# A four-layer attention stack on one core: the order of 2673 tasks from a written list instead of from a ranked greedy planner

## The chip, the cores and the metric

One core of a Trainium2 chip runs the whole program. The metric is the device time of one execution in microseconds (us). Engines are named as in the profile: PE is the matrix engine (PEld its weight loads), DVE the vector engine, ACT the scalar engine with its function tables, POOL the GpSimd engine, SP the engine that issues most transfers.

## The reference, cut to what matters

Four attention layers follow one another on a batch of 4 sequences of 256 rows by 256 columns, float32; the context `ctx` is a second input of the same size.

```python
# layer 0, twice: heads of 128, 16 heads, one learned extra key and value
h = layer_norm(x); q, k, v = h @ wq + bq, ctx @ wk + bk, ctx @ wv + bv      # 256 x 2048 each
x = x + softmax(q k^T / sqrt(128)) v @ wo + bo
x = x + gelu(layer_norm(x) @ w_fc1 + b_fc1) @ w_fc2 + b_fc2                 # 256 -> 1024 -> 256
# layer 1: 16 heads of 16 over ctx, then an MLP with tanh-gelu
# layer 2: the latents are x, keys and values from ctx and x (512 keys), 16 heads of 16, a mask, rms norm, MLP
# layer 3: 32 query heads of 8 over 8 key heads, a mask, projection, layer norm -> out
```

The four sequences (batches b = 0 to 3) depend on one another nowhere; within a batch everything is a chain.

## The kernel before, in words

The kernel is written as a list of tasks. `Task` (line 174) is one short stretch of PE work (or none), followed by its `posts`: pieces of work on DVE, ACT, POOL or SP that read what PE left in PSUM, each with an estimated duration. A task names what it comes `after`, and the buffers that it `takes` from and `gives` back to rings (`Ring`, line 144). The ring `PS` (line 198) holds the eight PSUM banks, shown in the profile as `ps_pj`, `ps_s`, `ps_et` and `ps_o`, two of each. There are 2673 tasks, 1547 of them with PE work.

PE work has three shapes. "full" uses the whole array. "rows" (queries against keys with heads of 16 or 8) uses 32 rows of the array for each matmul, and a task fills two of the four row strips; two such tasks with different strips can be issued as a pair, interleaved, so that four matmuls run side by side. "cols" (weights times values of those heads) uses 32 columns each, four at a time.

Stages, in the names of the code:

- Stage 0, layer 0. `norm` (line 246: statistics on DVE, a power on POOL as `root`, `apply` on DVE), `transposed`, then for four groups of four heads: `seven` (line 1090, the projections, each 2x2 block product done with seven products instead of eight, in four PE tasks `first` to `fourth`, with sums of operands made ahead on POOL: `sums`, `value_sums`, `wo_sums`), `scores` with a maximum on DVE and an exponential on ACT, `quotients` (line 1468: one reciprocal and four scalings of the tile `E` on DVE), `turns` (transposes of `E` with a copy by ACT to `eT`), `weighted` (to `cT`), `tile_sums` (line 1532: four additions on `cT` and `sc`, on DVE or POOL) and `products` (line 1547, the output projection: the first task `t1` needs no `tile_sums`, the second, `t2`, does), each added to the tile `X` by DVE.
- Stages 1, 3 and 5: the MLPs. `up` needs a GELU table in ACT, everything else of ACT the EXP table.
- Stages 2, 4: layers 1 and 2 (`unit16`, line 670): `maxima` (rows, with a DVE maximum into the tile `shift`), `turns`, `weights` (rows, with exponentials on ACT), `weighted` (cols), `ending`.
- Stage 6: layer 3 (`unit8`, line 579): `scores` (rows, with a DVE operation that adds the mask and takes the maximum), `exps` on ACT, `turns` with a copy by ACT or DVE, `weighted`, `ending`, projection, and `closing` (line 923: statistics, root, two DVE operations, the output transfer).

`plan` (line 1728) walks through the tasks once in Python, before the program is built, with one clock for each engine. At each step it looks at all tasks whose predecessors are done and whose buffers are free, ranks them by the longest remaining chain less handicaps by batch and by kind (`HANDICAPS`, line 1852) and takes the best of those that would start soonest. It pairs two "rows" tasks where it can. For a post that may go to either of two engines it takes the one that would end first. The steps are then emitted in that order (line 1892), and `Pinned` (line 126) keeps every engine's instructions in the order of emission: nothing is reordered later. On the chip each engine works through its own list in order, and waits only for data and for buffers. Since all instructions pass through `Pinned`, they all carry line 134 in the profile; tiles tell them apart.

The lines that keep DVE and POOL apart in the plan: a post marked `near` that lands on DVE is made longer by the time for which POOL is busy.

Of the kernel before, what the change touches and what calls it, by code (L numbers as in the profile page):

```python
# [51 lines left out]
def kernel(ctx: ExitStack, tc: tile.TileContext, a: dict, out: bass.AP):  # L52
# [193 lines left out]
    def norm(b, after, src, eps, mean, st, take=()):  # L246
# [39 lines left out]
        t = Task(b, None, 0, None, [t], posts=[Post(("POOL",), 300, root)], lag=0.1)  # L286
# [77 lines left out]
    def attention(L, b, after, hTs, dst, dst_after, weights_at, before):  # L364
# [214 lines left out]
        def unit8(t, q):  # L579
            u = {}  # L580
            S_tasks, V_tasks = [], []
            for j in range(4):
# [5 lines left out]
                for pair in range(2):  # L588
# [12 lines left out]
                    def least(e, i, v=v):  # L601
# [10 lines left out]
                        b, "rows", 0.87, scores, [grab], takes=takes, pair=pair,  # L612
# [6 lines left out]
                    for i in range(2):  # L619
# [5 lines left out]
                        def turns(i=i, v=v):  # L625
                            for kc in range(2):
# [10 lines left out]
                                b, "full", 0.49, turns, [tx], takes=[(PS, v, ("t", i))],  # L637
# [32 lines left out]
        def unit16(t, q):  # L670
# [3 lines left out]
            for g in range(2):  # L674
                Ms = []
                grab = Task(b, None, 0, None, ready[t], takes=[(SHIFTS[g], q["shift"], g)])
                for q0 in range(0, 2, per):
                    for pair in range(2):
# [13 lines left out]
                        def most(e, i, g=g, q0=q0, pair=pair, v=v):  # L692
# [8 lines left out]
                                b, "rows", 0.87, maxima, [grab], pair=pair,  # L701
# [24 lines left out]
            for kc in range(NCK):  # L726
# [5 lines left out]
                for pair in range(2):  # L732
# [13 lines left out]
                    def exps(e, i, kc=kc, pair=pair, v=v):  # L746
# [7 lines left out]
                            b, "rows", 0.87, weights, [grab], pair=pair, takes=[(PS, v, 0), (PS, v, 1)],  # L754
# [168 lines left out]
    def closing(b, after):  # L923

        for i in range(2):
# [20 lines left out]
            t = Task(b, None, 0, None, [t], posts=[Post(("POOL",), 300, root)], lag=0.1)  # L946
# [143 lines left out]
    def seven(b, after, A, sum_, block, T, to, bias, row=None):  # L1090
# [62 lines left out]
        def last(gives):  # L1153
# [18 lines left out]
        t2 = Task(b, "full", 0.86, second, [t1], takes=[(UU, u, 1), (HALFWAY, u, "in")], posts=saved(1, 0, 1, 0))  # L1172
        t3 = Task(
            b, "full", 1.73, third, [t2], takes=[(PS, v, 2), (UU, u, 2)],
# [3 lines left out]
            b, "full", 1.73, fourth, [t3], gives=[(HALFWAY, u, "in")],  # L1178
# [47 lines left out]
    for li in range(2):  # L1226
# [35 lines left out]
        for hg in range(NG):  # L1262
# [54 lines left out]
            for bp in range(2):  # L1317
# [112 lines left out]
                for bb in range(2):  # L1430
# [46 lines left out]
                    for h in range(HG):  # L1477
# [3 lines left out]
                        def turns(h=h, v=v, E=E):  # L1481
# [8 lines left out]
                            b, "full", 0.44, turns, tN, takes=[(PS, v, "pt"), (ET, y, "eT")],  # L1490
# [41 lines left out]
                    def tile_sums(e, c=c, sc=sc):  # L1532
# [11 lines left out]
                        posts=[Post(("DVE", "POOL"), {"DVE": 1400, "POOL": 3100}, tile_sums, near=True)],  # L1544
# [15 lines left out]
                    def add(i, j, at_, b=b, v=v, gives=()):  # L1560
                        def run(e):
                            to = Xb(b)[:, i, j * P : (j + 1) * P]
                            ve.tensor_tensor(to, v["pt"][2][:, at_ * P : (at_ + 1) * P], to, ALU.add)

                        return Post(("DVE",), 215, run, gives=gives)

                    t1 = Task(
                        b, "full", 0.88, products((0, (0, 0), (0, 0), True), (1, (0, 1), (1, 0), False)),
                        tC + [t_w["wo"], t_plus[b]], takes=[(PS, v, "pt")], posts=[add(0, 0, 0), add(0, 0, 1)],
                    )  # L1570
                    t2 = Task(b, "full", 0.44, products((0, 0, 0, False)), [t1, t_sc, t_tw], posts=[add(1, 0, 0)])

                    t3 = Task(
                        b, "full", 0.88, products((0, (1, 0), (0, 1), False), (2, 1, 1, False)), [t2],
# [3 lines left out]
                        b, "full", 0.88, products((0, 2, (1, 1), False), (2, (1, 1), 2, False)), [t3],  # L1578
# [136 lines left out]
    for t in reversed(tasks):  # L1715
        t.level = t.us + sum(p.us for p in t.posts) + t.lag + 0.25
        t.level += max((n.level for n in t.then + t.hinted), default=0.0)
    TURN = {"full": 0.1, "rows": 0.2, "cols": 0.14}
    LATE, TABLE, HELD = 0.2, 1.3, 1.0
    TAIL = {"DVE": 0.085, "ACT": 0.12, "POOL": 0.1, "SP": 0.0}  # L1720
    rings = {r for t in tasks for r, _, _ in t.takes} | {r for t in tasks for r, _, _ in t.gives}
    needs = {}
    for t in tasks:
        needs[t] = {}
        for r, _, _ in t.takes:
            needs[t][r] = needs[t].get(r, 0) + 1

    def plan(handicap):

# [4 lines left out]
        table, shape, held = EXP, None, False  # L1734
# [3 lines left out]
        by_batch, by_kind, (near, slack, solo, wide) = handicap  # L1738
        rank = {t: t.level - by_batch[t.stage][t.b] - by_kind.get((t.stage, t.kind), 0) for t in tasks}
        order = {t: i for i, t in enumerate(tasks)}  # L1740
        count = {t: len(t.after) + len(t.behind) for t in tasks}
        open_ = [t for t in tasks if not count[t]]
        ready = {t: 0.0 for t in open_}

        def earliest(t):

            if held and any(p.table not in (None, table) for p in t.posts):
                return None
            when = ready[t]
            for r, n in needs[t].items():  # L1750
                w = r.when(n)
                if w is None:
                    return None
                when = max(when, w)
            return when

        def do(group, start):
            nonlocal table, shape, held
            taken = []
            for t in group:  # L1760
                for r, h, k in t.takes:
                    h[k] = r.take()
                    taken.append((r, h, k, h[k][1]))
            end = start
            if group[0].shape:
                end = start + max(t.us for t in group)
                clock["PE"], shape = end, group[0].shape
                end += LATE
# [5 lines left out]
            for t, p in queue:  # L1774
                def ends(e):
                    more = TABLE if e == "ACT" and p.table not in (None, table) else 0.0
                    begin = max(clock[e], end)
                    if p.near and e == "DVE":
                        more += HELD * min(max(clock["POOL"] - begin, 0.0), p.ns[e])
                    return begin + more + p.ns[e] * wide  # L1780
# [11 lines left out]
            for t in group:  # L1792
                t.done += t.lag
                for r, h, k in t.gives:
# [3 lines left out]
                held = held if t.holds is None else t.holds  # L1798
                open_.remove(t)
                for n in t.then:  # L1800
                    count[n] -= 1
                    if not count[n]:
                        open_.append(n)
                        ready[n] = max([d.done + near for d in n.after], default=0.0)
            steps.append((group, taken, behind))

        def wait(t, w):
            switch = any(p.table not in (None, table) for p in t.posts)
            return max(w - clock["PE"], 0.0) + (TABLE / 2 if switch else 0.0)

        while open_:
            found = [(t, earliest(t)) for t in open_]
            found = [(t, w) for t, w in found if w is not None]
            if not found:
                return None
            best, products = None, []
            for t, w in found:
                if not t.shape:
                    continue
                turn = TURN[t.shape] if t.shape != shape else 0.0  # L1820
                idle = wait(t, w) + turn
                if t.shape != "rows":
                    products.append((idle, max(w, clock["PE"]) + turn, [t]))
                    continue
                for o, v in found:
                    if o.shape != "rows" or o.pair == t.pair or o.pair < t.pair:
                        continue
                    both = [w, v]
                    for r, n in needs[t].items():
                        both.append(r.when(n + needs[o].get(r, 0)))  # L1830
                    if None in both:
                        continue
                    both = max(both)
                    products.append((max(wait(t, both), wait(o, both)) + turn, max(both, clock["PE"]) + turn, [t, o]))
                products.append((idle + solo, max(w, clock["PE"]) + turn, [t]))
            if products:
                least = min(p[0] for p in products) + slack
                best = max((p for p in products if p[0] <= least), key=lambda p: (max(rank[t] for t in p[2]), -p[0]))
            others = [
                (max(w, clock["PE"], *(clock[p.engines[0]] for p in t.posts if p.engines[0] in ("POOL", "SP"))), -rank[t], order[t], t, w)  # L1840
                for t, w in found if not t.shape
            ]
            if others and (best is None or min(others)[0] <= best[1]):
                _, _, _, t, w = min(others)
                do([t], w)
            else:
                do(best[2], best[1])
# [4 lines left out]
    HANDICAPS = (  # L1852
        [
            [527, 717, 992, -701],
            [-9576, 3530, 999, -8122],
            [355, 669, -1239, 5671],
            [542, 1381, -2079, 2561],
            [-979, -2578, -4331, 417],
            [-1355, 7177, 208, -5575],
            [-677, -12218, 4083, 3351],  # L1860
        ],
        {
            (0, "columns.run"): -45, (0, "columns.scaled"): -58, (0, "context_sums.run"): -13,
            (0, "differences.run"): 122, (0, "exp"): 23, (0, "fetch.run"): -18, (0, "learned"): -54,
            (0, "norm.apply"): 29, (0, "norm.root"): 408, (0, "norm.stats"): 49, (0, "plus_row_to.run"): 12,
            (0, "products.run"): 9, (0, "quotients"): 13, (0, "rest_of.<lambda>"): -54, (0, "rows_of.<lambda>"): 65,
            (0, "run"): 3, (0, "scores"): 124, (0, "seven.first"): -1, (0, "seven.fourth"): 416,
            (0, "seven.second"): 124, (0, "seven.third"): 11, (0, "sums.run"): 2572, (0, "tile_sums"): 12,
            (0, "transposed.run"): -596, (0, "turns"): -615, (0, "value_sums.run"): 74, (0, "weighted"): 1704,
# [92 lines left out]
```

## Time and profile before

| | |
|---|---|
| median of 3 runs | 1338.98 us (1338.95 to 1340.37) |
| the profiled execution's own time | 1339.38 us |
| its span, first to last instruction | 1337.6 us |
| outside the span | 1.8 us |
| PE busy | 1300.0 us, 97% of the span |
| DVE busy | 873.2 us, 65% |
| ACT busy | 706.4 us, 53% |
| POOL busy | 266.0 us, 20% |
| granted PE clock | 0.999 |
| moved from and to HBM | 38.08 MB, mean 28 GB/s |

The profiled execution is 0.4 us above the median. The ends of matmuls are modelled and overlap the next ones, so that PE shows as busy in part of the time in which it is held up; the starts of matmuls tell more. A float32 matmul has two records in the trace, a transpose one, so 5143 instructions give 8907 records. The records of each engine stand in the order of the list, so every one of them can be put to its task.

### The profile page before, as it was taken

Reading aid. Unit: us, or ns where it says so; the run is one execution under the profiler, and the core shown is the slowest. Engines: PE = TensorE matmul, PEld = TensorE weight load, DVE = VectorE, ACT = ScalarE, POOL = GpSimd, SP = SyncE. Lnnn points to the kernel's source line nnn. Section 1 sums busy time; section 2 is a strip of 40 time slices with the busy share of each in tenths; the row PEclk is TensorE's granted clock in tenths of the full one; section 3 lists DMA queues with packets and bytes.
Section 4 is the critical chain, followed back from the end, with each engine's and each line's share of the span. In section 5 each row is a group of like instructions: output and inputs, shape, how many; then the busy total and the mean of one; then the engine's idle time right before and its main releaser. Section 6 shows DMA issues by size and latency. Waiting matters only on the chain.

```text
span 1337.6 us, 23607 instructions
## 1 busy us (share of the span) xinstructions
PE 1300.0 (97%) x8907; PEld 1038.3 (78%) x8907; DVE 873.2 (65%) x2431; ACT 706.4 (53%) x1689; POOL 266.0 (20%) x447
## 2 busy tenths in 40 slices
PE   8899999999999999999999999999999999999997
PEld 4788888888978888888898876658666667576764
DVE  6867757776687667676672577571772376556786
ACT  3554544544444535455363145545435687668986
POOL 8500304003241040120114341101220110020000
PEclk9999999999999999999999999999999999999999
DMA  7110200102001011010014110000000000000000
GB/s 235 33 32 1 79 1 17 64 1 79 1 16 64 1 35 46 1 48 1 11 59 142 39 49 5 1 1 5 5 5 1 1 1 1 17 1 9 2 9 17
DMA packets 25633, 38.08 MB, mean 28 GB/s; under 512 B 2244, under 2 KB 16086, under 8 KB 25392
## 3 DMA queue, kind: packets, MB, share of 16 engines
q1 hardware_dynamic: 24640, 35.56, 8.3%
q0 software_dynamic: 608, 0.76, 0.5%
q8 instruction: 70, 1.15, 0.4%
q14 instruction: 43, 0.35, 0.1%
q10 hardware_dynamic: 272, 0.26, 0.1%
HBM read 35.52 MB, written 1.05 MB: 27 GB/s over the span
## 4 chain that ended last, share of the span: by engine, by line
PE 86%; DVE 9%; ACT 3%; issue 1%; DMA 1%; SPq 0%; POOL 0%; DVEq 0%; ACTq 0%
PE ps_pj L134 22%; PE ps_et L134 22%; PE ps_s L134 21%; PE ps_o L134 21%; DVE E L134 1%; DVE eq L134 1%; ACT eq L134 1%; DMA bvl<-in_cols_dram 1%; DVE sc L134 1%; DVE qk L134 1%; ACT qk L134 1%; DVE X L134 1%; DVE shift L134 1%; DVE u L134 0%; ACT e L134 0%
## 5 line engine op out<-in xcount | busy, mean ns | idle before, releaser
L134 ACT ACTIVATE eq<-eq,nm 128x256 f32<-128x256 f32 x256 | 106.2, 505 | 0.0
L134 DVE TENSOR_SCALAR E<-E,rinv 128x257 f32<-128x257 f32 x256 | 96.6, 440 | 2.2
L134 PE MATMUL ps_s<-qk 32*128 32x256 f32 (+1 forms) x282 | 81.6, 474 | 1.0 <-ACT qk L134 0.6
L134 PE MATMUL ps_o<-qk 32*128 32x256 f32 (+1 forms) x270 | 76.5, 456 | 0.4 <-ACT qk L134 0.4
L134 POOL TENSOR_TENSOR X<-X,rowbc 128x256 f32<-128x256 f32 x56 | 41.3, 757 | 157.2 <-PE ps_et L134 69.6
L134 PE MATMUL ps_et<-qk 32*128 32x256 f32 (+1 forms) x258 | 70.8, 449 | 0.0
L134 PE MATMUL ps_pj<-qk 32*128 32x256 f32 (+1 forms) x214 | 63.0, 460 | 0.0
L134 POOL TENSOR_SCALAR mv<-mv 128x2 f32<-128x2 f32 (+1 forms) x32 | 7.5, 235 | 238.8 <-DVE mv L134 238.3
L134 DVE TENSOR_REDUCE shift<-ps_s 128x1 f32<-128x512 f32 (+1 forms) x62 | 41.8, 684 | 11.7 <-PE ps_s L134 5.0
L134 PE MATMUL ps_o<-eq,qk 32*128 32x256 f32 x216 | 47.3, 401 | 0.8 <-ACT e L134 0.8
L134 PE MATMUL ps_pj<-eq,qk 32*128 32x256 f32 x196 | 47.9, 401 | 0.0
L134 PE MATMUL ps_et<-eq,qk 32*128 32x256 f32 x204 | 47.0, 401 | 0.2 <-DVE qk L134 0.2
L134 PEld LDWEIGHTS ps_o<-qk 32*128 32x128 f32 x270 | 36.4, 183 | 8.6 <-issue 4.2
L134 PEld LDWEIGHTS ps_s<-qk 32*128 32x128 f32 x282 | 36.8, 183 | 7.8 <-issue 3.2
L134 POOL COPY kT<-lks 128x4 f32<-128x4 f32 x32 | 7.0, 234 | 170.1 <-PE ps_s L134 65.9
L134 PE MATMUL ps_s<-kT,qT 128*128 128x257 f32 x140 | 40.5, 382 | 0.0
L134 DVE TENSOR_TENSOR X<-ps_s,X 128x128 f32<-128x128 f32 (+2 forms) x86 | 25.6, 308 | 22.7 <-PE ps_s L134 21.3
L134 POOL TENSOR_TENSOR sc<-cT 128x256 f32<-128x256 f32 x18 | 13.5, 751 | 129.4 <-ACT cT L134 106.1
L134 PE MATMUL ps_o<-eT,V 128*128 128x256 f32 x152 | 39.1, 380 | 0.0
L134 ACT ACTIVATE cT<-ps_o,cols 128x256 f32<-128x256 f32 x37 | 17.5, 473 | 39.7 <-PE ps_o L134 39.6
L134 PE MATMUL ps_s<-eq,qk 32*128 32x256 f32 x152 | 38.3, 402 | 0.0
L134 DVE TENSOR_REDUCE shift<-ps_et 128x1 f32<-128x512 f32 (+1 forms) x47 | 31.8, 683 | 9.7 <-PE ps_et L134 8.1
(613 smaller groups left out, 4042.4 us busy)
## 6 DMA issues: line engine op xcount, KB each, us to landing
wk<-in_L_xattn_wk_dram SPq DMA_DIRECT2D x8, 512.0 KB, 3.6
wv<-in_L_xattn_wv_dram SPq DMA_DIRECT2D x8, 512.0 KB, 4.2
wq<-in_L_xattn_wq_dram SPq DMA_DIRECT2D x8, 512.0 KB, 5.5
wo<-in_L_xattn_wo_dram SPq DMA_DIRECT2D x8, 512.0 KB, 3.8
bvb<-in_bv_dram SPq DMA_DIRECT2D x8, 256.0 KB, 5.8
bvl<-in_cols_dram SPq DMA_DIRECT2D x8, 256.0 KB, 5.8
f<-in_L_xattn_w_fc_dram SPq DMA_DIRECT2D x2, 1024.0 KB, 5.0
f<-in_L_xattn_mlp_w_dram SPq DMA_DIRECT2D x2, 1024.0 KB, 5.9
```

The lines of the kernel that those rows point to most:

```text
L134: return lambda *args, **more: tc.keep_in_program_order(f(*args, **more))
```

## The change

The greedy search in `plan` goes. In its place stands `ORDER`, a written list of task numbers in which a pair of numbers in brackets is a pair of "rows" tasks. `plan` now only follows the list: it still assigns buffers and still chooses the engine of each post that has a choice, by its clocks. Bookkeeping tasks (no PE work, no posts, no buffers taken) are done as soon as they can be. The ranks, the handicaps, and the factor 1.11 by which every post was stretched in the plan are gone. Several estimated durations are changed. The tasks themselves, their arithmetic, buffers and dependences are the same.

```diff
-        t = Task(b, None, 0, None, [t], posts=[Post(("POOL",), 300, root)], lag=0.1)
+        t = Task(b, None, 0, None, [t], posts=[Post(("POOL",), 1000, root)], lag=0.1)
...
-                        b, "rows", 0.87, scores, [grab], takes=takes, pair=pair,
+                        b, "rows", 0.95, scores, [grab], takes=takes, pair=pair,
...
-                                b, "full", 0.49, turns, [tx], takes=[(PS, v, ("t", i))],
+                                b, "full", 0.44, turns, [tx], takes=[(PS, v, ("t", i))],
...
-                            b, "rows", 0.87, maxima, [grab], pair=pair,
+                            b, "rows", 1.04, maxima, [grab], pair=pair,
...
-                            b, "full", 0.44, turns, tN, takes=[(PS, v, "pt"), (ET, y, "eT")],
+                            b, "full", 0.48, turns, tN, takes=[(PS, v, "pt"), (ET, y, "eT")],
...
-                        posts=[Post(("DVE", "POOL"), {"DVE": 1400, "POOL": 3100}, tile_sums, near=True)],
+                        posts=[Post(("DVE", "POOL"), {"DVE": 1830, "POOL": 3500}, tile_sums, near=True)],
...
-    LATE, TABLE, HELD = 0.2, 1.3, 1.0
+    LATE, TABLE, HELD, NEAR = 0.2, 1.3, 1.0, 0.06
...
-    def plan(handicap):
+    def plan(order):
...
-        def do(group, start):
+        def do(group):
+            start = max([d.done + NEAR for t in group for d in t.after], default=0.0)
+            if group[0].shape:
+                start = max(start, clock["PE"])
...
-                    return begin + more + p.ns[e] * wide
+                    return begin + more + p.ns[e]
...
-        while open_:
-            found = [(t, earliest(t)) for t in open_]
...
+        for group in order:
+            do([tasks[i] for i in (group if isinstance(group, tuple) else (group,))])
...
-    HANDICAPS = (
...
+    ORDER = (
+        13, 47, 9, 54, 12, 2, 48, 51, 63, 3, 61, 64, 29, 22, 23, 49, 52, 30, 24, 31, 62, 25, 56, 28, 11, 35, 33, 226,
...
+        1573, 1564, 1565, 1566, 1536, 1567, 1554, 1581, 1555, 2399, 1577, (1578, 1579), (1582, 1583), 1569, 1570,
...
-    for group, taken, behind in plan(HANDICAPS)[1]:
+    for group, taken, behind in plan(ORDER)[1]:
```

Laid side by side, the two built programs differ as follows. The skeleton of stages and batches is nearly the same, and a PE task is moved by 2.3 us of PE work in the median (a tenth of them by more than 10.2 us), but of 1418 neighbours in the order of PE only 208 are kept.

| | before | after |
|---|---|---|
| steps with PE work: full, rows, cols | 1211, 128, 80 | 1211, 131, 80 |
| pairs of "rows" tasks, single ones | 128, 0 | 125, 6 |
| changes of shape along PE's order | 317 | 301 |
| loads of ACT's tables | 14 | 16 |
| `tile_sums` on DVE, on POOL | 23, 9 | 9, 23 |
| `differences` on DVE, on POOL | 5, 1 | 2, 4 |
| `context_sums` on DVE, on POOL | 2, 2 | 0, 4 |
| subtraction `bvb` less `bvl` on DVE, on POOL | 8, 0 | 1, 7 |
| copies after `turns` of layer 3 on ACT, on DVE | 98, 30 | 82, 46 |

In SP's list for the first group of heads, the second half of `ctx` and of `x` moves ahead of the weights' tail: `ctx` from the 17th to the 8th transfer, `x` from the 16th to the 12th, while `wq` falls behind `bvb` and `bvl`.

## The prediction

> **What bounds the kernel now.** I read the page first, its busy times and slices.
>
> ```profile
> PE 1300.0 (97%) x8907; PEld 1038.3 (78%) x8907; DVE 873.2 (65%) x2431; ACT 706.4 (53%) x1689; POOL 266.0 (20%) x447
> PE   8899999999999999999999999999999999999997
> DVE  6867757776687667676672577571772376556786
> ACT  3554544544444535455363145545435687668986
> PE 86%; DVE 9%; ACT 3%; issue 1%; DMA 1%; SPq 0%; POOL 0%; DVEq 0%; ACTq 0%
> ```
>
> PE is the bound: 97% busy, 86% of the chain that ended last. The change leaves PE's arithmetic alone, so it can only win time in which PE stands. ACT nears its limit in the last eighth of the span, where its digits are 8 and 9. Next, PE in order of time, for what one step costs.
>
> ```profile
> 33.28 1.03 PE L134 MATMUL ps_s<-craw,wq 128*128 128x256 f32 x4
> 34.14 0.60 PE L134 MATMUL ps_et<-ident,xn 128*128 128x128 f32 x4
> ...
> 1300.74 0.38 PE L134 MATMUL ps_s<-w3o,oT 128*128 128x256 f32 x1
> 1301.05 0.48 PE L134 MATMUL ps_pj<-qk 32*128 32x256 f32 x2
> 1301.37 0.38 PE L134 MATMUL ps_pj<-qk 32*128 32x256 f32 x2
> 1301.59 0.38 PE L134 MATMUL ps_pj<-qk 32*128 32x256 f32 x2
> 1301.81 0.38 PE L134 MATMUL ps_pj<-qk 32*128 32x256 f32 x2
> 1302.13 0.48 PE L134 MATMUL ps_s<-w3o,oT 128*128 128x256 f32 x1
> ```
>
> Starts, not lengths, give the step: 34.14 - 33.28 over 4 is 0.215 us for 128x256. Into a "rows" step it is 0.31 (1300.74 to 1301.05), out of one 0.32: a change of shape costs about 0.09. A pair of "rows" tasks takes 1.08 (1301.05 to 1302.13), four waves.
>
> I then took every start-to-start interval of PE beyond the usual one for its two shapes. These excesses sum to 78.2 us: 8.5 in the first twentieth of the span, 31.2 in the last four (7.9, 6.3, 5.3, 11.7). Of the 78.2, pieces under 150 ns make 34.6 and larger ones 43.6. The first matmul starts at 4.8 us (ctx landing) and 6.7 us follow the last start. The larger pieces are what an order can remove. The wait list and one of the largest pieces show how they arise.
>
> ```profile
> PE ps_s L134 <- DVE u L134: 3.3, 4, 2.1
> PE ps_s L134 <- DVE X L134: 2.3, 5, 1.0
> PE ps_pj L134 <- DVE E L134: 1.5, 1, 1.5
> ```
>
> ```profile
> 387.39 3.08 DVE L134 TENSOR_SCALAR E<-E,rinv 128x257 f32<-128x257 f32 x4
> 387.94 0.77 POOL L134 TENSOR_TENSOR f<-wk 128x256 f32<-128x256 f32 x1
> ...
> 390.59 2.22 DVE L134 TENSOR_SCALAR E<-E,rinv 128x257 f32<-128x257 f32 x3
> ...
> 391.33 0.55 PE L134 MATMUL ps_pj<-ident,E 128*128 128x128 f32 x3 [1.51 <-DVE E L134]
> ```
>
> ```profile
> L134 DVE TENSOR_SCALAR E<-E,rinv x256: 339/349/909, 42.7 to 691.4; 128x257 f32<-128x257 f32 x128
> ```
>
> The four scalings of `quotients` took 3.08 us where the median of 0.349 makes 1.4, and PE stood 1.51. In the trace 47 of the 256 scalings are over 450 ns, and all 47 overlap a POOL instruction. So DVE is slowed by POOL beside it, and then PE waits for DVE.
>
> **Part by part**, against the profiled execution, 1339.4 us (span 1337.6 and 1.8 around it).
>
> *PE's own work.* 16 changes of shape fewer, by 0.093 (309 against 216 ns between starts): -1.5. Three more "rows" steps, since six tasks run alone: a lone task has the same four waves of about 0.22 us with half the array idle, 3 x 0.87 = +2.6. Sum +1.1; ends -1.5 (lone waves free) and +1.7 (3 x 1.08 - 1.5).
>
> *PE's waits.* Three counts on the two orders, with PE steps and post durations at the trace's typical values for their kind.
> - PE steps, past the first 60 us, that come too early even if every queue were empty: 39 before, 15 after (-62%). The shortfalls sum to 19.1 and 2.4 us; in layer 2 (stage 4) alone 9.5 becomes 0.
> - Those with under 1 us to spare: 231 before, 180 after (-22%).
> - Work listed for DVE or ACT beyond 20 us in any 20 us of PE work, up to 1100 us of it: 7.5 + 5.6 before, 6.2 + 2.5 after (-34%).
>
> Their mean is -39%; of 43.6 us that is -17.1. The ends are -22% (-9.6) and -62% (-27.0). One row speaks for less. Before's steps that came too early had 0.18 us of excess each, those with 1.5 to 2 us to spare still 0.12; class by class this gives only -4.9. I keep -4.9 for the range and take the mean, because large pieces need a late producer and a long queue at once, which the classes do not see. In the last 124 us of PE work ACT's load falls from 218% to 203% of a 62 us half (9.3 us) and DVE's rises from 188% to 196%; that is part of the same 43.6, not added.
>
> *ACT's tables.* Two more loads at 1.283 us (14 in the trace) fall near 1101 us of PE work, around one MLP's second half, where ACT is listed at 94%. What waits behind them are exponentials, and PE for those. 0 if hidden, 2.6 if not; I take +1.3, as that window has 6% to spare.
>
> *POOL for DVE.* To POOL go 14 `tile_sums` (four additions of 0.73 and gaps, 3.2), 7 subtractions of 512 columns (no row on POOL; twice 0.73, so 1.5), 3 `differences` (3.0) and 2 `context_sums` (2.1): 45 + 10 + 9 + 4 = 68 us. DVE loses 14 x 1.96 + 7 x 0.86 + 3 x 1.56 + 2 x 1.87 = 42 us. What waits for a `tile_sums` is the second product `t2`. From the last `weighted` to it lie 4.8 to 24.3 us of PE work in all 23 cases on POOL (before: 3.1 to 13.5 on DVE), against 3.2 needed; behind one `sums` in POOL's queue (3.2 more) the shortest is 1.6 late. The price is in what runs beside it. The scalings were 256 x (0.440 - 0.349) = 23.3 us too long beside 266 us of POOL; 334 us make that 29.3, +6.0 us on DVE. DVE is 65% busy and PE waits for a third of such delays at most: +2. Upper end: work of the slowed sort fills 154 of about 690 us of stage 0 on DVE, 22%; 22% of 68 is 15 us, all of it on PE. Lower end 0: a POOL instruction shortens none on DVE, and the freed DVE time is already in the waits.
>
> A rule of the Trainium skill speaks against this move: in SBUF — State Buffer, section "Who interferes with whom", the port pair that DVE and GpSimd share is an exclusive lock, and the later instruction waits for the whole of the other. The 909 ns maximum beside a 349 ns median agrees with a wait behind one POOL instruction. Taken at its worst, it would make this item +15 rather than +2, and the total 13 us later.
>
> *The head.* After, both `apply` steps of the first norms stand behind the subtraction that needs `bvl`. That landed at 16.14 (3.85 + 12.29 in the chain); half a megabyte (`wq`) ahead of it goes, 1.3 to 2.1 us at 235 to 380 GB/s, so about 14.4. With 0.86 + 2 x 0.73 the transposes start near 16.8, when PE would be ready at 14.4: 2.4 of wait against 1.3 now. In return `x`'s second half, issued at 18.93 before, is issued earlier, and the wait of 1.8 at 46.9 for a norm can go. Sum about 0; ends -4 and +3.
>
> *The end.* `stats` of the first half moves between the two last additions: its root starts about 0.2 us earlier. -0.2.
>
> Sum: 1.1 - 17.1 + 1.3 + 2 + 0 - 0.2 = -12.9, so 1326.5 by the profiled execution and, 0.4 lower, 1326 by the median.
>
> **The rivals.**
> - *The waits go deeper.* The list suits DVE, ACT and PSUM at once, and of 43.6 only 7 us remain: 1339 - 36 + 1 = 1304. For it: 9.5 to 0 in stage 4. Against: DVE plus ACT in the last 124 us are listed at 399% of a half against 406%, nearly as full.
> - *Only the classes' gain.* Waits move rather than go: -4.9 + 1.1 + 1.3 + 2 = -0.5, 1338.5. For it: excess hardly follows spare time in before's trace. Against: the falls in all three counts.
> - *Slower, by the port.* Added POOL work lengthens `quotients` and additions in stage 0 for PE in full, +15, and the waits fall by 4.9 only: 1.1 - 4.9 + 1.3 + 15 = +12.5, 1351; with -9.6 it is 1347. It decides once over half of the 68 us meets DVE work that PE is waiting for. For it: 386 to 391 us. Against: `tile_sums` on POOL have 4.8 us or more, and DVE's list gets 28 us shorter in stage 0.
> - *The list does nothing.* Excluded: only 208 of 1418 neighbours on PE stay.
>
> **How the numbers follow.** Forecast 0.55, with a range of its own of 1313 (waits at -27) to 1334 (at -9.6); deeper 0.13; classes only 0.15; slower 0.17. A measurement of this kernel can tell 0.2%, 2.7 us. Half of "classes only" is a gain over that, the rest no change: faster 0.55 + 0.13 + 0.08 = 0.76, same 0.07, slower 0.17. The range runs from 1304, the deeper case, to 1345, leaving out the worse half of the slower case.
>
> **What would show it.** PE's starts: excess near 61 us, large pieces near 27. Stage 4 and the last eighth should gain most; scalings of `E` over 450 ns should be more than 47. If POOL decides, PE's waits "<- DVE E" and "<- DVE u" grow and the slices of stage 0 get longer. If tables decide, ACT shows two loads near 1180 us and PE waits for ACT `e` beside them. I am wrong if the larger pieces are not fewer.

## The result and the profile after

The kernel with the written list takes 1319.55 us (median of 4 runs, 1319.4 to 1320.68) against 1339.67 us before (4 runs, 1338.95 to 1341.14): ratio 0.985, 95% interval 0.9833 to 0.9867. The gain is 20.1 us where 12.9 were forecast. The span fell from 1337.6 to 1317.7 us.

The page of after: busy times, three rows of slices, and the chain that ended last.

```profile
PE 1289.4 (98%) x8907; PEld 1040.5 (79%) x8907; DVE 852.5 (65%) x2380; ACT 692.1 (53%) x1659; POOL 321.0 (24%) x530
PE   8999999999999999999999999999999999999997
DVE  4866665676787566666674457582664386747788
ACT  2545444543535444454453255545334786678886
...
PE 92%; DVE 5%; ACT 1%; issue 1%; DMA 0%; POOL 0%; DVEq 0%; POOLq 0%; ACTq 0%
```

PE's share of the chain rose from 86% to 92%, and DVE's fell from 9% to 5%: what went are places where PE stood for DVE. POOL has 55 us more to do, DVE 21 us less. The number of PE records is the same.

The starts of PE's matmuls say where the time went. Both traces are measured here by the usual intervals of before.

| | before, us | after, us | difference |
|---|---|---|---|
| PE's excess over the usual intervals | 78.2 | 60.8 | -17.4 |
| ... its pieces of 150 ns and more | 43.7 | 29.7 | -14.0 |
| ... its pieces below that | 34.5 | 31.1 | -3.4 |
| the usual intervals themselves | 1247.9 | 1245.8 | -2.1 |
| from PE's last start to the end | 6.7 | 6.3 | -0.4 |
| start of the first matmul | 4.8 | 4.8 | 0 |

By the kind of step, from its first start to the next step's: "rows" steps of all layers together -3.1 us (2.3 of it in stage 4, 0.7 in stage 2); of the other steps stage 6 (layer 3) -6.3, stage 0 -3.9, stage 2 -3.4, stage 4 -1.3, the MLPs -1.6. In the last eighth of the span the excess fell from 20.2 to 12.3 us.

Not all waits fell. The largest entries of PE's list of waits (what waited, for what: us in total, times, longest) are, after its first transfer, these:

```profile
PE ps_o L134 <- DVE E L134: 2.3, 2, 1.3
PE ps_s L134 <- DVE E L134: 1.8, 2, 1.3
PE ps_pj L134 <- DVE X L134: 1.8, 3, 0.8
PE ps_pj L134 <- DVE E L134: 1.3, 2, 0.9
```

With one more of 0.8 us, the waits for `E`, the tile that `quotients` scales, make 6.2 us, where before had 1.5; those for `u` fell from 4.7 to 0.6. The list cured one kind of late producer and left, or made, another. Two of these waits stand next to each other:

```profile
143.46 0.72 POOL L134 TENSOR_TENSOR f<-wv 128x256 f32<-128x256 f32 x1
...
144.27 0.73 POOL L134 TENSOR_TENSOR t<-wv,f 128x256 f32<-128x256 f32 x1
...
144.32 3.17 DVE L134 TENSOR_SCALAR E<-E,rinv 128x257 f32<-128x257 f32 x4
...
147.61 3.03 DVE L134 TENSOR_SCALAR E<-E,rinv 128x257 f32<-128x257 f32 x4
...
148.44 0.63 PE L134 MATMUL ps_s<-ident,E 128*128 128x128 f32 x4 [1.29 <-DVE E L134]
...
149.98 0.63 PE L134 MATMUL ps_o<-ident,E 128*128 128x128 f32 x4 [0.91 <-DVE E L134]
```

Eight scalings take 0.79 and 0.76 us each, at the pace of POOL's weight sums beside them (one every 0.80 us), where the median is 0.349. PE stands 1.29 and 0.91 us for them. The other waits for `E` also stand behind slowed scalings: four between 46 and 66 us (3.4 us together) and one at 236 us (0.5). The longest of all, at 49 us, stands beside work that the change itself put on POOL, the subtraction `bvb` less `bvl`:

```profile
45.93 3.35 DVE L134 TENSOR_SCALAR E<-E,rinv 128x257 f32<-128x257 f32 x4
...
47.09 1.31 POOL L134 TENSOR_TENSOR bvb<-bvb,bvl 128x512 f32<-128x512 f32 x1
...
49.34 0.55 PE L134 MATMUL ps_o<-ident,E 128*128 128x128 f32 x3 [1.35 <-DVE E L134]
```

### The profile page after: what moved, and what is told of

Its sections match the earlier page's. It is cut to its first block, busy times and chain, and to the rows that moved or that the text cites. A ratio compares the mean times of both kernels' runs of the same rounds, so it can differ in the third digit from the quotient of the medians.

```text
span 1317.7 us, 23581 instructions
## 1 busy us (share of the span) xinstructions
PE 1289.4 (98%) x8907; PEld 1040.5 (79%) x8907; DVE 852.5 (65%) x2380; ACT 692.1 (53%) x1659; POOL 321.0 (24%) x530
## 4 chain that ended last, share of the span: by engine, by line
PE 92%; DVE 5%; ACT 1%; issue 1%; DMA 0%; POOL 0%; DVEq 0%; POOLq 0%; ACTq 0%
PE ps_o L134 25%; PE ps_s L134 23%; PE ps_et L134 22%; PE ps_pj L134 22%; DVE E L134 2%; ACT qk L134 1%; DVE qk L134 1%; DMA rows<-in_cols_dram 0%; DVE eq L134 0%; DVE u L134 0%; DVE X L134 0%; ACT E L134 0%; DVE craw L134 0%; DVE kT L134 0%; DVE V L134 0%
## 5 line engine op out<-in xcount | busy, mean ns | idle before, releaser
L134 POOL TENSOR_TENSOR sc<-cT 128x256 f32<-128x256 f32 x46 | 33.8, 734 | 232.6 <-ACT cT L134 164.2
L134 PE MATMUL ps_pj<-qk 32*128 32x256 f32 (+1 forms) x272 | 73.2, 450 | 0.0
L134 PE MATMUL ps_s<-qk 32*128 32x256 f32 (+1 forms) x246 | 70.2, 453 | 0.4 <-ACT qk L134 0.4
L134 PE MATMUL ps_s<-eq,qk 32*128 32x256 f32 x192 | 45.2, 400 | 0.0
L134 DVE TENSOR_REDUCE shift<-ps_o 128x1 f32<-128x512 f32 (+1 forms) x52 | 35.1, 682 | 12.9 <-PE ps_s L134 6.4
L134 ACT ACTIVATE E<-ps_s,nm 128x257 f32<-128x257 f32 x65 | 30.8, 475 | 23.7 <-DVE nm L134 23.7
L134 PE MATMUL ps_et<-kT,qT 128*128 128x257 f32 x140 | 41.4, 382 | 0.5 <-DVE kT L134 0.5
L134 ACT ACTIVATE E<-ps_o,nm 128x257 f32<-128x257 f32 x62 | 29.5, 476 | 22.6 <-DVE nm L134 22.6
L134 ACT ACTIVATE E<-ps_et,nm 128x257 f32<-128x257 f32 x70 | 33.1, 474 | 15.4 <-DVE nm L134 15.1
L134 PEld LDWEIGHTS ps_pj<-qk 32*128 32x128 f32 x272 | 35.9, 184 | 6.0 <-issue 3.8
```

The lines of the kernel that those rows point to most:

```text
L134: return lambda *args, **more: tc.keep_in_program_order(f(*args, **more))
```

## Experiments

The theories: O, the list itself carries the gain, because it gives late producers more time; E, the other choice of engines does (more on POOL, less on DVE); C, the corrected durations do. Medians are given beside those of the kernel before on the same chip.

**1. The list with before's engines.** After's order and buffers, each of 190 posts on the engine that before chose for it.

```diff
-                e = min(p.engines, key=ends)
+                e = p.chosen if len(p.engines) > 1 else p.engines[0]
```

> The written list and the buffers of after, but every engine chosen as in before (162 tasks between ScalarE and VectorE, 28 between VectorE and GpSimd go back). Theory O (the order itself gives the gain, by spacing what PE needs): most of the 20.1 us stays, 1320 to 1328 us. Theory E (the other choice of engines relieves VectorE, and the order only follows it): near 1335 us, within 5 us of before. If both are fitted to one another, it lies between them.

Measured: 1368.23 against 1339.02 us, ratio 1.022 (1.0203 to 1.0237). Both theories missed: not a part of the gain stays, the list with strange engines is 48.7 us above after. The longest waits of PE include

```profile
PE ps_s L134 <- DVE sc L134: 4.1, 1, 4.1
```

`sc` is written by `tile_sums`, here on DVE in a place that the list filled for POOL.

**2. Before's order with after's engines.** The same edit the other way round.

> The order and the buffers of before, with the engines of after (the 190 choices). Theory O: no gain, 1339 us or up to 8 us above, since the engines were chosen for other neighbours. Theory E: near 1325 us.

Measured: 1380.42 against 1339.02 us, ratio 1.0309 (1.0294 to 1.0325). E is out: the choices bring nothing by themselves. O is right on the side and short in the size, since 41 us is far above the 8 that it allowed. Order and engines are one fit; neither can be tried without the other.

**3. Right durations without the list.** Before's planner and handicaps, after's durations.

```diff
-                        posts=[Post(("DVE", "POOL"), {"DVE": 1400, "POOL": 3100}, tile_sums, near=True)],
+                        posts=[Post(("DVE", "POOL"), {"DVE": 1830, "POOL": 3500}, tile_sums, near=True)],
...
```

> No written list: the planner of before makes its own list, with the handicaps of before, but with the durations of after in its plan. Theory C (the plan was wrong because its durations were, and right ones mend it): 1330 us or less. Theory O (a search over lists did it, and handicaps that were fitted to the old durations fit the new ones worse): 1339 to 1365 us; by the measured durations this list has 77 steps of TensorE that come before what they need is ready, where the one of before has 39.

Measured: 1409.54 against 1339.02 us, ratio 1.0532 (1.0516 to 1.0548). C is out in this form. The count of steps that come too early points the right way over three kernels: 15, 39 and 77 of them go with an excess of 60.8, 78.2 and 123.1 us (in after, before and this one). Not all of the 70 us are waits: the mean granted clock was 0.972 against 0.999, and 0.027 of 1407 us is an estimate of 38 us at most for that (see the last section).

**4 and 8. Half a list.** One kernel has after's list up to PE's last step of stage 0 and then before's order; the other is the reverse.

```diff
-    ORDER = (A)
+    ORDER = (A up to the last "full" step of stage 0, then what is left, as B has it)
```

> The list of after up to TensorE's last step of stage 0, and from there on the order of before, its engines too. If the gain sits in the later stages, as the excess of TensorE by stage shows it (stage 0 has 3.9 us of it, the others and the rows 15.6 us), some 1335 us. If the head and stage 0 carry it by what they leave behind for the later stages, near 1325 us.

> The other half of the split: the order and engines of before up to TensorE's last step of stage 0, and from there on after's. If the gain sits behind stage 0, as the split the other way round showed with 1336.4 us against 1339.0, it is 1323 to 1326 us. If the two halves only work together, 1330 us or more.

Measured: 1336.39 against 1339.02 us (ratio 0.9985, 0.9976 to 0.9995) for the early half, 1326.69 against 1339.56 us (0.9903, 0.989 to 0.9917) for the late half. That is 2.6 and 12.9 us, 15.5 of the 20.1 together; the other 4.6 are lost in cutting the list. The excess agrees: 74.8 and 66.3 us where before has 78.2. Most of the gain lies behind stage 0. In the profiled executions the loss is 2.9 us, and it lies in the MLP right behind the join: by the starts of its steps stage 1 takes 59.0 and 60.1 us there, where before has 58.3 and after 57.6.

**5. The 28 choices between DVE and POOL.** After, with these alone as before had them, which takes 60 us from POOL.

> After, with only the 28 pieces of work that it puts on GpSimd rather than VectorE (or the reverse) back where before has them; order, buffers and all choices between ScalarE and VectorE as in after. If GpSimd's work beside VectorE's scalings has its small price (+2 us in the sum): 1317 to 1318 us. If it has its heavy price (+15): 1305 to 1310 us. If the order is fitted to these choices and VectorE needs the relief: 1322 us or more, with TensorE's waits for VectorE longer.

Measured: 1338.5 against 1339.56 us, ratio 0.9984 (0.9975 to 0.9992). All of the gain but 1 us is gone, for DVE work of 26 us:

```profile
PE 1292.8 (97%) x8907; PEld 1038.9 (78%) x8907; DVE 878.6 (66%) x2463; ACT 693.2 (52%) x1659; POOL 261.5 (20%) x447
```

DVE is 66% busy instead of 65%, and ACT and PE have the same work. The profiled execution took 1334.55 us, 15.1 above after's, and its excess is 76.0 us against 60.8; of these 15.2 us, 14.5 lie in five of the first ten twentieths of the span, all in stage 0 (twentieths 4, 6, 7, 8 and 10: 21.2 us against 6.7). PE's list of waits shows for what:

```profile
PE ps_et L134 <- DVE X L134: 3.7, 3, 1.7
PE ps_s L134 <- DVE sc L134: 3.5, 1, 3.5
PE ps_pj L134 <- DVE sc L134: 2.2, 3, 1.1
```

All waits for `sc`, the output of `tile_sums`, come to 6.5 us where after has none, and those for `X` to 8.0 where after has 3.7. So POOL's share is no free extra of the change but a condition of this list, and the price of its work beside the scalings (PE's waits for `E` are 6.2 us in after and still 5.2 here) is much smaller than what it takes off DVE. The third reading of the expectation held. The other 4 us of the median go with the clock: the two executions with a clock of 0.999 took 1334.43 and 1334.55 us, those at 0.995 to 0.996 took 1338.5 to 1338.93.

**6. 14 table loads.**

```diff
-        ... 1990, ... (2534, 2535), ...
+        ... (2534, 2535), 1990, ...
```

> After, with one task (the first half of an up-projection of batch 1) moved behind its neighbours, so that ScalarE loads its tables 14 times and not 16. Priced as in the sum (1.3 us on the path): 1318.2 us. Hidden behind other work: 1319.5 us, no change. If the moved task was placed where it was for TensorE's sake: 1321 us.

Measured: 1325.65 against 1339.56 us (ratio 0.9898, 0.9883 to 0.9913). The profiled execution took 1320.96 us at a clock of 0.998; the three others took 1325.11 to 1327.15 us at 0.993 to 0.996. Two table loads are gone and nothing is won: PE gets a new wait near 1152 us,

```profile
PE ps_s L134 <- ACT eq L134: 2.5, 1, 2.5
```

ACT is late there with `eq`. The profiled execution is 1.5 us longer than after's, but up to 1153 us, where the two programs are the same, it is 1.6 us ahead; over the moved task, and one copy beside it that the plan now gives to ACT instead of DVE, it falls 1.5 us behind, so the move costs some 3.1 us there. After's four table loads of this stretch stand between 1156 and 1167 us, and in its trace no wait of PE is listed from 1140 to 1180 us. The two loads were hidden where they stood, and the moved task stood where it did for a reason.

**7. No single "rows" tasks.**

```diff
-        (1685, 1650), ... 1651, ...
+        (1651, 1650), ... (1685, 1652), ...
```

> After, with the six row-tiled tasks that run alone put together again in three pairs (128 pairs as in before, three steps fewer). If their price is that of the sum (2.6 us more TensorE work) and nothing is won by their standing alone: 1317 us. If they stand alone because a partner is not ready in time, the pairs wait and it is 1320 to 1323 us.

Measured: 1321.92 against 1339.56 us (ratio 0.9866, 0.9853 to 0.988), 2.4 us above after. Its profiled execution is 3.2 us longer than after's, and 1.6 us of that lie at 134 to 201 us, where no "rows" task stands and where the clock is 0.72 for 6 us; that part is not the pairs' doing. What is left there is a loss of 1.6 us, not a gain of 2.6. In after the six lone tasks take 4.9 us up to the next step's start, three usual pairs (1.08 each) 3.2, so standing alone does cost 1.7 us; but with them paired all "rows" steps together take 1.3 us longer, not shorter. The second reading of the expectation held: the pairs wait.

**9 and 10. The durations, with engines free to follow.** The plan chooses its engines by its clocks, so the fair exchange is of order and durations. Nine is after's list with before's durations, ten before's order with after's.

```diff
-    LATE, TABLE, HELD, NEAR = 0.2, 1.3, 1.0, 0.06
+    LATE, TABLE, HELD, NEAR = 0.2, 1.3, 1.0, 0.09
...
-                    return begin + more + p.ns[e]
+                    return begin + more + p.ns[e] * 1.11
```

> After's written list, with the durations of before in the plan (its factor 1.11 and its 0.09 too). The plan then differs from after's only in 58 of its choices between ScalarE and VectorE, in none between VectorE and GpSimd, and in which buffer of a ring it takes. Theory O (the list carries the gain, and the choices follow from it): 1320 to 1325 us. Theory C' (list and durations are one fit; the 162 such choices that were put back cost some 30 us, so 58 cost about a third): 1330 us or more.

> Before's order written as a list, with after's durations in the plan, which changes 35 of before's choices of an engine (2 of them to GpSimd) and its choice of buffers. If right durations choose better engines by themselves: 1330 to 1336 us. If they do nothing without the order: 1337 to 1341 us. If any change of choices in a fitted order costs, by the same third of a fit as above: 1343 to 1350 us.

| | durations of before | durations of after |
|---|---|---|
| order of before | 1339.7 | 1340.3; ratio 1.0004 (0.9995 to 1.0014) |
| list of after | 1323.0; ratio 0.9871 (0.9857 to 0.9886) | 1319.6; ratio 0.985 (0.9833 to 0.9867) |

This settles it. The list is worth 16.8 us with the old durations and 20.7 with the new; the durations are worth nothing without the list and some 3 us with it. Of these 3 us a part is the clock again: nine's executions took 1320.66 us at 0.998 and 1322.84 to 1323.14 at 0.996. The engines follow the list: nine differs from after in 58 choices, all between ACT and DVE, and in none between DVE and POOL.

**11. POOL's weight sums cut short.** What is left out is stated in the expectation.

```diff
+            if late:
+                A11, A12, A21, A22, S2, S3, S4 = (x[:, :, 0:4] for x in (A11, A12, A21, A22, S2, S3, S4))
             ge.tensor_tensor(S3, A11, A21, ALU.subtract)
```

> After, with the 72 GpSimd sums and differences of the query, key and value weights from the third set of weights on cut to 4 columns (their outputs are then incomplete; all waits and every other instruction stay). If the wait of VectorE's scalings of E behind GpSimd is what stops TensorE at 146.8 and 148.8 us, those two stalls (1.5 and 1.1 us) go and the scalings there fall from 0.79 to 0.35 us each: 1317 us, and 1313 us if all of the stalls for these scalings after 140 us go. If something else is late next: 1319 us. The scalings over 450 ns fall from 49 to about 25.

Measured: 1316.11 us (1315.12 to 1318.55), 3.4 below after. Scalings over 450 ns fell from 49 to 35 (about 25 was expected), what all scalings take beyond 345 ns from 25.1 to 18.4 us. The third twentieth of the span, with the stalls at 147 and 149 us, gains 2.5 us; the others move by up to 1.2 us either way. So of the sums that were cut, those at this place cost PE some 2.5 us, and the others fall on scalings that PE hardly waits for. The work of POOL before 70 us is left as it was here, and so are PE's waits for `E` there; what they would give is not tested.

**12. The same place mended.** The two POOL tasks that are due last in that set move behind `tile_sums`.

```diff
-        ... 410, ... 414, ... 313, ...
+        ... 313, 414, 410, ...
```

> After's list with two of its entries moved, the GpSimd work on the value weights and the value bias of the third set (tasks 414 and 410), behind the tile sums that GpSimd begins at 159 us; nothing else changes on any engine. GpSimd is then done with its weight sums near 147 us instead of 151. If its work is what slows the scalings of E there (0.79 us each instead of 0.35): the second group of four takes 1.4 us again, TensorE loses 1.5 to 2 us less at 147 to 150 us, and the time is 1317.5 to 1318. If something else is late next there: 1319.5 us. If the moved sums, due at 171 us and then ready near 168, stop TensorE: up to 1321 us.

Measured: 1317.12 us (1315.99 to 1317.87) against 1339.38, ratio 0.9833 (0.982 to 0.9846). No run of the five is as long as the shortest of after's four. The medians are 2.4 us apart, though the two ratios' intervals overlap; in the profiled executions the place itself gives 1.8 us. The same place in its timeline (everything in it is 1.7 us earlier; 1.5 of these come from the first twentieth, where the two programs are the same and the excess was 6.6 us instead of 8.1 in this execution):

```profile
142.64 2.70 DVE L134 TENSOR_SCALAR E<-E,rinv 128x257 f32<-128x257 f32 x4
...
144.46 0.73 POOL L134 TENSOR_TENSOR f<-wk,f 128x256 f32<-128x256 f32 x1
...
145.46 1.14 DVE L134 TENSOR_SCALAR E<-E,rinv 128x257 f32<-128x257 f32 x4
...
145.96 0.63 PE L134 MATMUL ps_s<-ident,E 128*128 128x128 f32 x4 [0.51 <-ACT cT L134]
...
146.49 0.63 PE L134 MATMUL ps_o<-ident,E 128*128 128x128 f32 x4
```

POOL is done with the weights at 145.2, the second group of scalings takes 1.14 us instead of 3.03, and the second wait of PE (0.91) is gone; the first is down from 1.29 to 0.51, now for `cT` of ACT. The excess of that twentieth fell from 2.9 to 1.1 us, as forecast.

## Why the prediction was right, and where its size was off

Direction and mechanism held: PE's larger stalls went, PE's arithmetic stayed, and the excess came to 60.8 us where "near 61" was said. That it comes so close is in part luck: the pieces of 150 ns and more fell by 14.0 us where 17.1 was taken (29.7 are left, "near 27" was said), and the smaller ones, which the sum left as they were, fell by 3.4. Against the sum:

| step | forecast, us | measured, us |
|---|---|---|
| PE's waits, ACT's tables and POOL for DVE | -17.1 + 1.3 + 2 = -13.8 | -17.4, all in PE's excess |
| PE's own work | +1.1 | -2.1 |
| the end | -0.2 | -0.4 |
| sum | -12.9 | -19.9 |

The steps that failed are these.

- *ACT's tables* (+1.3) cost nothing: in after's trace no wait of PE is listed beside the loads, and run 6 lost time without them.
- *POOL for DVE* (+2) had its size from the wrong place. The scalings took 24.4 us too long before and 25.1 after. The step reckoned them to grow by 6.0 us in proportion to POOL's time, of which it had 68 us more; POOL works 55 us more, and they grew by 0.7, for 64 scalings meet POOL's additions instead of 50, but each loses less (mean 723 ns against 815). Yet PE's waits for `E` grew by 4.7 us. Of these 3.7 are there in run 5 too, without the moved work: they come with the list, which puts slowed scalings where PE waits for them. The other 1.0 is what the moved work cost, and without it run 5 lost 15 us.
- *PE's own work* (+1.1) came to -2.1. Of the 2.6 us for three more "rows" steps 1.7 can be seen on the lone tasks (run 7), but the other "rows" steps became shorter: the intervals between "rows" matmuls, waits included, sum to 109.8 us after and 110.5 before. The changes of shape were undersized at -1.5: the usual intervals at changes fell by 4.4 us, while those between "full" matmuls grew by 1.0.
- *The head* came out near its sum of 0 (the excess of the first twentieth went from 8.5 to 8.1 us), but not by its terms: the subtraction that needs `bvl` began on DVE at 11.1 us, where `bvl` had been put at 14.4, and no wait of PE is listed at the transposes that were to wait 2.4 us.
- *Stage 4 should gain most* was wrong. The steps there that came too early had 9.5 us of shortfall in the count, and stage 4 gained 3.6 us with its "rows" steps (1.3 without), where stage 6 gained 6.3, stage 2 4.1 and stage 0 3.9. The mean of three counts fitted the whole kernel, and not its stages. The last eighth did gain most, 7.9 us.
- *The class-by-class count* (-4.9) was far too small; setting it aside was right. The reason given for it (a late producer and a long queue at once) fits run 5, where more work in DVE's queue alone brought waits back, but no run tried it by itself.
- Two slips in the working: with the waits at -27 alone the sum gives 1316.6, not 1313 (the lower end of the head, -4, would make up the rest), and ACT's last five digits are 6, 8, 9, 8 and 6.

Of the rivals, "slower by the port" named a cost that is there, and "<- DVE `E`" grew from 1.5 to 6.2 us as it said; yet "<- DVE `u`" fell, the scalings over 450 ns went only from 47 to 49, and stage 0 got 3.9 us shorter. Where it said that POOL's work costs, run 5 showed the reverse on balance for this list: without it 15 us are lost in stage 0. "Only the classes' gain" and "the waits go deeper" lie 19 us above and 15.6 us below the result.

The rule of the Trainium skill (SBUF — State Buffer, "Who interferes with whom") describes what the traces show at 144 to 151 us, each scaling held to POOL's pace of 0.80 us. It told the kind of the cost, not its amount: that depends on whether PE waits for that scaling, and in this list it does so at 46 to 66, at 147 to 150 and at 236 us.

What stays open: why a list gives late producers more time in one stage and not in another (the counts follow the excess over whole kernels, but not by stage), and how much of the 3.4 us between run 9 and after is the durations' and how much the clock's.

## What to carry to other kernels

Where an order is written out and engines are chosen along it, order and engines are one fit: test them by exchanging order and durations with the choice left free, since freezing one against the other cost 29 and 41 us here and said little on either. Ask of a cost first whether PE waits where it stands: two table loads here stood where it did not, and were worth nothing. After a search, look in the list of waits for what grew: two entries moved by hand gave another 1.8 us at the place they were moved for.

## What the runs showed of the hardware that was not expected

The mean granted clock of PE was lower in the slower kernels (0.991 to 0.992 in run 1, 0.968 to 0.972 in run 3, 0.997 to 0.999 in after), and the loss comes on top of the waits. In the windows of run 1 (us; busy us and records of PE, PEld, DVE, ACT, POOL; granted clock; DMA), PE waits 4.1 us for `sc` from 650.2 us on, and comes back at half the clock, which lasts 3.4 us:

```profile
650.00:652.00 2.00, 0.24 (x2) 0.00 (x0) 1.96 (x9) 0.00 (x0) 0.00 (x0) 1.00 0.00 0
652.00:654.00 2.00, 0.00 (x0) 0.00 (x0) 1.83 (x5) 0.00 (x0) 0.00 (x0) 0.97 0.00 0
654.00:656.00 2.00, 1.67 (x6) 1.58 (x7) 0.99 (x3) 0.00 (x0) 0.00 (x0) 0.50 0.00 0
656.00:658.00 2.00, 2.00 (x7) 1.65 (x7) 0.69 (x1) 0.00 (x0) 0.00 (x0) 0.67 0.00 0
658.00:660.00 2.00, 2.00 (x14) 1.86 (x14) 0.69 (x2) 0.59 (x1) 0.00 (x0) 1.00 0.00 0
```

A stop of 2.9 us at 1171 us of the same run left the clock at 1.00, while one of 2.1 us at 942 us in run 3 was followed by ten microseconds at 0.50. The Trainium skill (TensorE: Matmul & The Clock Gate, section 'Part 1: The HAM clock gate (the "warmup" mystery)') says that the clock is halved after an idle window of about 3.4 us that runs free of the program. The first two stops agree with that, the third does not. Nor does this stretch of run 3, where PE shows as busy throughout, no wait over 0.4 us is listed from 760 us on, and the clock stands at 0.50 for 20 us:

```profile
784.00:788.00 4.00, 3.93 (x29) 2.33 (x29) 4.00 (x9) 0.00 (x0) 2.11 (x3) 0.97 0.09 5
788.00:792.00 4.00, 4.00 (x18) 2.76 (x18) 3.60 (x8) 0.00 (x0) 0.05 (x1) 0.50 0.02 4
...
804.00:808.00 4.00, 4.00 (x37) 1.51 (x33) 0.00 (x0) 2.42 (x4) 0.00 (x0) 0.50 0.00 0
808.00:812.00 4.00, 3.66 (x40) 2.22 (x40) 0.00 (x0) 2.51 (x5) 0.00 (x0) 0.97 0.01 4
```

From 776 to 787 us PE issues mostly matmuls on 32 rows there; that these count for less is a guess that no run here tried, and before and after issue such matmuls too. In their profiled executions neither before nor after falls under 0.99 in any window of 6 us up to 1300 us. The dips also come in some executions of one stretch of a program and not in others: in run 7's profiled execution the clock is 0.50 for 3.4 us from 150.6 us on, right behind the two stops for `E`, where its list is still that of after, whose own profiled execution has no dip there. This is why the clock stands beside the times of runs 5, 6 and 9.
